# The inverse column transform of a spectral mix: half as many matmul columns, with two more levels of sums on VectorE and GpSimd

## The chip, the cores and the metric

The kernel runs on one core of one Trainium2 chip. A core has five engines that run side by side, each with its own instruction queue: TensorE (PE) for matmuls, VectorE (DVE), ScalarE (ACT) and GpSimd (POOL) for elementwise work, and SyncE (SP), which issues DMAs. They wait for each other through semaphores. The metric is the device time of one execution in microseconds; lower is better.

## The reference, cut to what matters

The input `x` is a float32 array of 16 batches, 16 channels and 256 x 256 points. Two layers follow each other, each behind a group normalisation and with a residual addition. The second is a stack of convolutions and a gate; the change doesn't touch it. The first is a layer in the frequency domain:

```python
alpha = jnp.fft.fft2(x, axes=(-2, -1))
...
S = jnp.einsum('ikpq,oikp,xikq->oxik', weights_residue, A, Bm)
output_residue1 = jnp.einsum('biox,oxik->bkox', alpha, S)
...
x1 = jnp.fft.ifft2(output_residue1, s=(Ny, Nx), axes=(-2, -1)).real
```

For every frequency (o, x) the 16 input channels are mixed into 16 output channels by a complex matrix `S`, which is made of poles and residues. The result goes back to space. The change lies in the part of the inverse transform that runs along x.

## The kernel before, in words

The program has four stages: `layer0_forward` (transform to frequencies), `layer0_mix` (the mix, and the way back along x), `layer0_back` (the way back along y, with the pole terms), and `layer1`. They pass arrays through DRAM: the mix reads the spectrum `al` and writes `hd`, which `layer0_back` reads.

All transforms are matmuls against tables of cosines and sines, made on the host as constants by `fourier_tables`. In `layer0_forward` the spectrum along x comes from the table `wxn`, in the mix the way back along x uses the table `ix`. Both belong together: they fix at which points in x the transform takes its origin.

`layer0_mix` works through 33 groups of four rows of frequencies (the last group has one row). Its order is written out by hand for PE, ACT, DVE and POOL; each of these engines carries out its instructions in the order of the program text. A group `g` goes like this:

- `poles` builds weights `lt` on DVE (L629) for the next group.
- `mix(s, y, between)`: for 256 frequencies in x, small matmuls (L665) of the matrices `s` with the spread spectrum `alb`, 8 blocks; ACT copies each block from PSUM to `y` (L672). At blocks 24 and 48 (`x0`) it carries on with the column transform of the row before, which was left over.
- Then for the rows f = 0 to 3 of the group: `turn` transposes `y` on PE (L681); half of the result is copied by DVE (L687), half by ACT (L685), to `yt`. `residues` makes the matrices `s` of the next group on PE (L643), copied by DVE (L651) and ACT (L653) in turn. `spread` multiplies the next spectrum into `alb`: the expansions, on DVE (L607: three for f = 0 to 2, one for f = 3) and ACT (L605: two for f = 0 to 2). Then `columns`, which the change rewrites. For f = 3 it is put off into the next mix loop.

The next mix can't begin before all of `s` and of `alb` are written. `alb` has one buffer, so its expansions begin after the mix that reads it.

`columns(g, f, yt)` takes the frequencies of one row and gives values at 256 points in x. The 16 batches are in two halves of lanes, q = 0 and 1, and the even and odd frequencies (e) are summed apart. For each e it has four products (real and imaginary input c; v) per half, accumulated in PSUM tile `ph[q]`: 16 matmuls with 256 columns each. In float32 each matmul is two instructions on PE in the profile, so 32 in a step. The first 128 points need even + odd, the other 128 even - odd: ACT copies the odd half out of PSUM (L709), DVE makes the sum (L712) and the difference (L713) into tile `h`, and POOL issues two DMAs that store `h` to `hd` (L720). The pool of `ph` has two buffers, that of `h` five.

Of the kernel before, what the change touches and what calls it, by code (L numbers as in the profile page):

```python
# [10 lines left out]
F32 = mybir.dt.float32  # L11
I32 = mybir.dt.int32
AF = mybir.ActivationFunctionType
ALU = mybir.AluOpType
# [5 lines left out]
N = 256  # L20
G = 8
P = 128
# [3 lines left out]
TWO_PI = 2.0 * np.pi  # L26
# [30 lines left out]
def load(nc, pool, src, shape, name):  # L57
    t = pool.tile(shape, F32, tag=name, name=name)
    nc.sync.dma_start(out=t, in_=src)
    return t  # L60
# [493 lines left out]
def layer0_mix(ctx, tc, d, al, hd, tabs):  # L554
# [3 lines left out]
    nc = tc.nc  # L558
    nb = d["x"].shape[0]
    cp = ctx.enter_context(tc.tile_pool(name="mc", bufs=1))  # L560
# [12 lines left out]
    for k in range(0, C, 4):  # L573
        nc.sync.dma_start(out=tt[:, :, k : k + 4], in_=tabs[0][:, :, k : k + 4])
    ident = load(nc, cp, d["ident"], [P, P], "ident")
    ix = load(nc, cp, d["ix"], [P, 8, N], "ix")

# [5 lines left out]
    hp = ctx.enter_context(tc.tile_pool(name="mh", bufs=3))  # L585
    psg = ctx.enter_context(tc.tile_pool(name="psg", bufs=4, space=PSUM))
    pst = ctx.enter_context(tc.tile_pool(name="pst", bufs=2, space=PSUM))
    psh = ctx.enter_context(tc.tile_pool(name="psh", bufs=2, space=PSUM))
# [85 lines left out]
    def turn(y, f):  # L674

        yt = hp.tile([P, 8, 8, C], F32, tag="yt", name="yt", bufs=2)
        for t0 in range(0, 8, 4):
            pt = pst.tile([P, 4, P], F32, tag="pt", name="pt")
            for t in range(4):
                j = 16 * f + 2 * (t0 + t)  # L680
                nc.tensor.transpose(pt[:, t], y[:, j : j + 2].rearrange("p q x -> p (q x)"), ident)  # L681
            dst = yt[:, :, t0 : t0 + 4].rearrange("p c t k -> p t c k")
            src = pt.rearrange("p t (c k) -> p t c k", k=C)
            if t0:
                nc.scalar.copy(dst, src)  # L685
            else:
                nc.vector.tensor_copy(dst, src)  # L687
        return yt

    def columns(g, f, yt):  # L690

        ph = [psh.tile([P, 2, N], F32, tag="ph", name="ph") for q in range(2)]
        for e in range(2):
            if e:
                yield
            for n, (c, v) in enumerate(((0, 0), (0, 1), (1, 0), (1, 1))):
                i = 2 * (2 * c + e) + v
                for q in range(2):
                    lanes = slice(64 * q, 64 * q + 64)
                    nc.tensor.matmul(  # L700
                        ph[q][:, e],
                        lhsT=yt[lanes, i].rearrange("p t k -> p (t k)"),
                        rhs=ix[lanes, i],
                        start=n == 0,
                        stop=n == 3,
                    )
        for q in range(2):
            odd = hp.tile([P, 2, P], F32, tag="odd", name="odd", bufs=2)
            nc.scalar.copy(odd, ph[q][:, 1].rearrange("p (v x) -> p v x", v=2))  # L709
            o = hp.tile([P, 2, 2, P], F32, tag="h", name="h", bufs=5)  # L710
            even = ph[q][:, 0].rearrange("p (v x) -> p v x", v=2)
            nc.vector.tensor_tensor(o[:, :, 0], even, odd, ALU.add)  # L712
            nc.vector.tensor_tensor(o[:, :, 1], even, odd, ALU.subtract)  # L713
            o = o.rearrange("p v h x -> p v (h x)")
            fy = 4 * g + f
            for v in range(2):

                if fy % P or v == 0:
                    part = fy // P if fy % P == 0 else v
                    nc.gpsimd.dma_start(  # L720
                        out=hd[fy % 2, part, fy % P // 2, q:nb:2].rearrange("b k x -> b (k x)"),
                        in_=o[:, v],
                    )

    E = mybir.EngineType
    with tc.manual_schedule(engines={E.PE, E.Activation, E.DVE, E.Pool}):
# [3 lines left out]
        s = gp.tile([P, N, 2, C], F32, tag="s", name="s")  # L730
# [7 lines left out]
        for g in range(NF):  # L738
            more = g + 1 < NF
            y = gp.tile([P, 64, 64], F32, tag="y", name="y")  # L740
            if more:
                lt = poles(av)
            mix(s, y, between)
            if more:
                s = gp.tile([P, N, 2, C], F32, tag="s", name="s")
                residues(lt, s, 0)
            for f in range(4 if more else 1):
                if more and f == 3:
                    spread(spectrum, f)
                    for k0 in (12, 14):  # L750
                        residues(lt, s, k0)
                yt = turn(y, f)
                if more:
                    for k0 in range(2 if f == 0 else 4 * f, 4 * f + 4, 2) if f < 3 else ():
                        residues(lt, s, k0)
                    if f < 3:
                        spread(spectrum, f)
                    if g + 2 < NF:
                        if f == 0:
                            av = load_poles(g + 2)  # L760
                        spectrum[f] = load_spectrum(g + 2, f)
                between = columns(g, f, yt)
                if f < 3:
                    for _ in between:
                        pass
# [642 lines left out]
def fourier_tables():  # L1408

    k = np.arange(N)  # L1410
    turns = np.outer(k, k) % N * (TWO_PI / N)
    cos, sin = np.cos(turns), np.sin(turns)

    def parities(a):
        return a.reshape(P, 2, *a.shape[1:])


    fy = np.stack([np.stack([cos[:P, e::2][:, :64], -sin[:P, e::2][:, :64]], 1) for e in (0, 1)], 1)
    fy[:, 0, 1, 0] = cos[:P, P]
    wx = np.stack([cos, -sin, sin], axis=1)  # L1420

    wxn = np.stack(
        [
            np.stack([np.concatenate([cos[:P, e::2], -sin[:P, e::2]], 1),
                      np.concatenate([sin[:P, e::2], cos[:P, e::2]], 1)], axis=1)
            for e in (0, 1)
        ],
        axis=1,
    )

    ix = np.stack([np.concatenate(a, 1) for a in ((cos[:, :P], sin[:, :P]), (-sin[:, :P], cos[:, :P]))], 1)
    ix = np.tile(ix.reshape(64, 8, N), (2, 1, 1))

    iy = np.stack([cos[:P], -sin[:P]], axis=1) / (N * N)
    iy[0, 0] *= 0.5
    iy[0, 1] = 0.5 * cos[P] / (N * N)
    number = (k + P) % N - P
    mirrored = -number[-k % N]
    ii, tt = np.arange(C), np.arange(2)

    mt = np.zeros((2, C, M, 2, 2, 8))
    for t in tt:
        for i in ii:
            mt[t, i, :, i // 8, t, i % 8] = 1
    out = {
        "fy": fy.reshape(P, 2, P),
        "wx": parities(wx),
        "wxa": parities(wx[..., :P]),
        "wxn": wxn,
        "ix": ix,  # L1450

        "iy": iy[..., :P].reshape(64, 2, 2, P).transpose(2, 0, 1, 3).reshape(P, 2, P),
        "ones": np.full((P, P), 1.0 / P),
        "pair": np.stack([np.tile(np.eye(64), (2, 1)), -np.tile(np.eye(64), (2, 1))], axis=1),
        "gc": np.tile(np.repeat(np.eye(G), 2, axis=0), (8, 1)),
        "ident": np.eye(P),
        "kcol": parities(number),
        "krow_t": np.repeat(np.stack([number, mirrored]), 64, axis=0),
        "krow_m": np.tile(np.repeat(np.stack([number, mirrored]), 32, axis=0), (2, 1)),
        "sign_t": np.repeat([-1.0, 1.0], 64)[:, None],  # L1460
        "sign_m": np.tile(np.repeat([-1.0, 1.0], 32), 2)[:, None],
        "mk": np.tile(np.repeat(np.eye(C), M, axis=0), (2, 1)),
        "m4": np.tile(np.repeat(np.eye(4), 8, axis=0), (4, 1)),
        "m8": np.tile(np.repeat(np.eye(8), M, axis=0), (4, 1)),
        "mt": mt.reshape(P, 2, 16),
        "phase": np.repeat([0.25, 0.0], 64)[:, None],
        "last": np.repeat([0.5, -0.5], 64)[:, None] / (N * N),
    }
    return {name: a.astype(np.float32) for name, a in out.items()}
# [70 lines left out]
```

## Time and profile before

| what | value |
|---|---|
| median of 3 runs | 7066.57 us (7063.95 to 7071.69) |
| profiled execution, its span | 7064.8 us |
| busy, share of the span | PE 93%, DVE 79%, ACT 54%, POOL 50% |
| mean granted PE clock | 0.976 |
| mix, first to last group of four rows | 1413 to 2880 us |
| L700, matmuls of `columns` | 4128 instructions, 509.6 us busy, 393 ns mean |
| L712 and L713, sum and difference | 258 each, medians 425 and 415 ns |
| L709, copy on ACT | 258, median 378 ns |
| L607, expansions on DVE | 330, median 1392 ns |
| L720, store issues on POOL | 512, median 596 ns |

The span is the time from the first to the last instruction of the one execution that the profiler recorded; 1.8 us lie between it and the median. [...] "Idle before, releaser" tells what an engine waited for; "issue" stands for a wait in which the profile sees no releaser. Lines such as L700 are lines of the program.

### The profile page before, as it was taken

The numbers are of one execution on the slowest core, as the hardware profiler recorded it, in microseconds if no ns is written. First come the engines' busy times: TensorE is split into PE (matmuls) and PEld (weight loads), VectorE is DVE, ScalarE is ACT, GpSimd is POOL, SyncE is SP. The second block draws the span as 40 slices with busy tenths as digits, with TensorE's granted clock in tenths as the row PEclk, the third lists the DMA queues.
The fourth block names the chain that finished last, engine by engine and source line by source line (L and its number), as shares of the span: only waits on it lengthen the run. The fifth ranks groups of instructions, "written<-read, shape, count | busy, mean of one in ns | idle before, by whom it ended". The sixth has DMA issues, their size and how long they took to land. (4 is left out here: it accounts for less than half of the span.)

```text
span 7064.8 us, 144662 instructions
## 1 busy us (share of the span) xinstructions
PE 6544.4 (93%) x55592; PEld 3663.8 (52%) x55592; DVE 5610.5 (79%) x10346; ACT 3836.7 (54%) x5996; POOL 3516.5 (50%) x4614
## 2 busy tenths in 40 slices
PE   7889999899999999899979999999999999999996
PEld 5777778677677677677723333333333333333331
DVE  8999985466666666688878888888888888888885
ACT  1223333366666666322266666676666666666671
POOL 2334445412222222466655666667666667665663
PEclk9899999999999999999989999999999999999998
DMA  3334444433333333699968888899888889888886
GB/s 97 112 114 124 121 126 124 131 96 97 96 102 99 100 95 100 211 326 327 326 188 251 261 257 267 277 277 286 272 258 265 275 276 285 270 260 264 279 271 212
DMA packets 716083, 1443.41 MB, mean 204 GB/s; under 512 B 98954, under 2 KB 525254, under 8 KB 673638
## 3 DMA queue, kind: packets, MB, share of 16 engines
q1 hardware_dynamic: 567206, 959.76, 44.3%
q0 software_dynamic: 148192, 474.40, 21.4%
q8 instruction: 444, 7.27, 0.4%
q14 instruction: 241, 1.97, 0.1%
HBM read 877.12 MB, written 556.47 MB: 203 GB/s over the span
## 5 line engine op out<-in xcount | busy, mean ns | idle before, releaser
L1087 ACT ACTIVATE wide<-c,b 32x512 f32<-32x512 f32 x2176 | 1477.5, 679 | 312.8 <-PE c L1039 264.1
L1118 DVE TENSOR_TENSOR top<-pd,t 32x512 f32<-32x512 f32 x2176 | 1504.3, 691 | 52.5
L1039 PE MATMUL c<-z,w 102*128 102x512 f32 x2048 | 999.5, 620 | 110.5 <-ACT wide L1087 89.0
L1115 DVE TENSOR_TENSOR t<-pd,r 64x512 f32<-64x512 f32 x1088 | 744.4, 684 | 349.6 <-PE pd L1107 311.9
L1099 POOL COPY wide<-wide 32x1031 f32<-32x1031 f32 (+1 forms) x576 | 577.9, 1003 | 886.8 <-ACT wide L1087 859.7
L1107 PE MATMUL pd<-wide,dw 128*128 128x512 f32 x2048 | 990.9, 605 | 12.0 <-DVE top L1118 11.0
L720 POOL DMA_DIRECT2D hd<-h x512 | 323.3, 638 | 1192.5 <-DVE h L713 1169.0
L1039 PEld LDWEIGHTS c<-z,w 102*128 102x128 f32 x2048 | 371.7, 192 | 697.5 <-issue 460.1
L1187 PE MATMUL c2ps<-rows,c 128*32 128x512 f32 x6144 | 721.8, 602 | 5.6 <-DVE odd L1214 5.6
L1107 PEld LDWEIGHTS pd<-wide,dw 128*128 128x128 f32 x2048 | 381.8, 192 | 572.5 <-issue 420.2
L1058 ACT ACTIVATE bot<-c,b 128x512 f32<-128x512 f32 x544 | 344.0, 683 | 464.5 <-issue 382.7
L1100 POOL COPY wide<-wide 32x1031 f32<-32x1031 f32 (+1 forms) x576 | 576.9, 1002 | 33.5
L700 PE MATMUL ph<-ix,yt 64*128 64x256 f32 x4128 | 509.6, 393 | 10.7 <-issue 9.9
L643 PE MATMUL ps<-tt,lt 128*64 128x256 f32 x4224 | 493.2, 384 | 10.4 <-DMA tt<-td 9.2
L313 PE MATMUL px<-wxn,u 128*64 128x256 f32 x4224 | 481.6, 379 | 8.0 <-ACT o L320 8.0
L207 PE MATMUL pu<-fy,eo 128*128 128x128 f32 x2048 | 428.6, 293 | 25.4 <-DVE u L224 21.3
L700 PEld LDWEIGHTS ph<-ix,yt 64*128 64x128 f32 x4128 | 397.0, 191 | 99.3 <-issue 51.3
L1187 PEld LDWEIGHTS c2ps<-rows,c 128*32 128x32 f32 x6144 | 175.9, 108 | 513.5 <-issue 402.3
L875 POOL TENSOR_TENSOR x<-x,o 128x512 f32<-128x512 f32 x256 | 324.0, 1266 | 217.8 <-DVE o L874 199.8
L607 DVE TENSOR_SCALAR alb<-alc,m 128x1024 f32<-128x1024 f32 x330 | 419.6, 1395 | 0.0
L214 PE MATMUL pv<-at,eo 128*128 128x128 f32 x2048 | 415.5, 286 | 0.0
L651 DVE COPY s<-ps 128x512 f32<-128x512 f32 x264 | 266.3, 1027 | 183.3 <-PE ps L643 166.3
(220 smaller groups left out, 11728.0 us busy)
## 6 DMA issues: line engine op xcount, KB each, us to landing
rows<-cf SPq DMA_DIRECT2D x128, 2176.0 KB
z<-zn SPq DMA_DIRECT2D x768, 257.8 KB
cf<-top POOLq DMA_DIRECT2D x512, 240.0 KB, 6.8
cf<-bot POOLq DMA_DIRECT2D x96, 840.0 KB, 11.0
alc<-al SPq DMA_DIRECT2D x264, 256.0 KB
zn<-zb SPq DMA_DIRECT2D x128, 516.0 KB
o<-zn SPq DMA_DIRECT2D x128, 516.0 KB
z<-in_x SPq DMA_DIRECT2D x64, 1024.0 KB
```

The costliest lines, as they stand in the source:

```text
L207: nc.tensor.matmul(pu[:, xh, e].rearrange("p v m -> p (v m)"), lhsT=lhs, rhs=fy[:, e], start=True, stop=True,)
L313: nc.tensor.matmul(ps[64 * k : 64 * k + 64, :, h], lhsT=u[:, h, part, g0 + j + k].rearrange("p f c -> p (f c)"), rhs=wxn[:, h, part], star ...
L643: nc.tensor.matmul(ps[64 * h : 64 * h + 64, v], lhsT=lt[:, h, k, 1 - v : 3 - v].rearrange("p l f c -> p (l f c)"), rhs=tt[:, h, k], start= ...
L700: nc.tensor.matmul(ph[q][:, e], lhsT=yt[lanes, i].rearrange("p t k -> p (t k)"), rhs=ix[lanes, i], start=n == 0, stop=n == 3,)
L1039: nc.tensor.matmul(ps[:, a], lhsT=w, rhs=z[:k, c : c + 2, 0:N], start=True, stop=True)
L1087: nc.scalar.activation(self.feat[64 - 32 * q : 96 - 32 * q, f, self.groups[g], :H], ps[q][32 * f : 32 * f + 32], AF.Mish, bias=b1[0][32 * ...
L1099: nc.gpsimd.tensor_copy(flat[0:32, f, 1:m], flat[64:96, f, 0 : m - 1])
L1100: nc.gpsimd.tensor_copy(flat[96:128, f, 0 : m - 1], flat[32:64, f, 1:m])
L1107: nc.tensor.matmul(ps, lhsT=dwt if self.tail else dw, rhs=self.feat[:, f, cs, :H], start=True, stop=True,)
L1115: nc.vector.tensor_tensor(t[64:128], ps[:64], self.r[:, cs], ALU.mult)
L1118: nc.vector.tensor_tensor(self.top[32 * f : 32 * f + 32, cs, q], ps[lanes], t[lanes], ALU.add)
L1187: nc.tensor.matmul(ps[32 * j : 32 * j + 32], lhsT=w[:, blk], rhs=src[:, 4 * j + blk : 4 * j + blk + 4, x : x + H], start=(i, blk) == (0, 0 ...
```

## The change

The way back along x is now taken on a grid moved by half a sample. The forward table `wxn` uses the angles of (2k + 1) instead of 2k, and `ix` likewise. On such a grid, the points x and 255 - x are mirror images: the cosine part has the same value at both, and the sine part the opposite one. The points x and x + 128 still differ only in the sign of the odd frequencies. So `ix` needs 64 points instead of 128, with a block of cosines and one of sines.

The matmuls of `columns` have 128 columns instead of 256. They are as many as before, each output now takes two products instead of four, and the output goes into two of four blocks of 64 in `ph` for each e: blocks 0 and 3 for v = 0, blocks 1 and 2 for v = 1. ACT copies the antisymmetric blocks (`anti`). DVE makes `w`: symmetric + antisymmetric, and symmetric - antisymmetric, the latter written backwards in x. POOL, which did nothing but issue the stores here, then makes the sum and the difference over e into `h`: two instructions for each half. The stores stay. The tile `w` is new (three buffers of 2 KB a partition), and `ix` has half its size.

```diff
-    ix = load(nc, cp, d["ix"], [P, 8, N], "ix")
+    ix = load(nc, cp, d["ix"], [P, 8, P], "ix")
...
-        ph = [psh.tile([P, 2, N], F32, tag="ph", name="ph") for q in range(2)]
+        ph = [psh.tile([P, 2, 4, 64], F32, tag="ph", name="ph") for q in range(2)]
         for e in range(2):
             if e:
                 yield
-            for n, (c, v) in enumerate(((0, 0), (0, 1), (1, 0), (1, 1))):
-                i = 2 * (2 * c + e) + v
-                for q in range(2):
-                    lanes = slice(64 * q, 64 * q + 64)
-                    nc.tensor.matmul(
-                        ph[q][:, e],
-                        lhsT=yt[lanes, i].rearrange("p t k -> p (t k)"),
-                        rhs=ix[lanes, i],
-                        start=n == 0,
-                        stop=n == 3,
-                    )
+            for v in range(2):
+                blocks = slice(0, 4, 3) if v == 0 else slice(1, 3)
+                for c in range(2):
+                    i = 2 * (2 * c + e) + v
+                    for q in range(2):
+                        lanes = slice(64 * q, 64 * q + 64)
+                        nc.tensor.matmul(
+                            ph[q][:, e, blocks],
+                            lhsT=yt[lanes, i].rearrange("p t k -> p (t k)"),
+                            rhs=ix[lanes, i].rearrange("p (b x) -> p b x", b=2),
+                            start=c == 0,
+                            stop=c == 1,
+                        )
         for q in range(2):
-            odd = hp.tile([P, 2, P], F32, tag="odd", name="odd", bufs=2)
-            nc.scalar.copy(odd, ph[q][:, 1].rearrange("p (v x) -> p v x", v=2))
-            o = hp.tile([P, 2, 2, P], F32, tag="h", name="h", bufs=5)
-            even = ph[q][:, 0].rearrange("p (v x) -> p v x", v=2)
-            nc.vector.tensor_tensor(o[:, :, 0], even, odd, ALU.add)
-            nc.vector.tensor_tensor(o[:, :, 1], even, odd, ALU.subtract)
-            o = o.rearrange("p v h x -> p v (h x)")
+            anti = hp.tile([P, 2, 2, 64], F32, tag="anti", name="anti", bufs=2)
+            nc.scalar.copy(anti, ph[q][:, :, 2:])
+            w = hp.tile([P, 2, 2, 2, 64], F32, tag="w", name="w")
+            sym = ph[q][:, :, :2]
+            nc.vector.tensor_tensor(w[:, 0], sym, anti, ALU.add)
+            nc.vector.tensor_tensor(w[:, 1, :, :, ::-1], sym, anti, ALU.subtract)
+            o = hp.tile([P, 2, 4, 64], F32, tag="h", name="h", bufs=5)
+            parts = o.rearrange("p v s x -> p s v x")
+            nc.gpsimd.tensor_tensor(parts[:, 0::3], w[:, :, 0], w[:, :, 1], ALU.add)
+            nc.gpsimd.tensor_tensor(parts[:, 2:0:-1], w[:, :, 0], w[:, :, 1], ALU.subtract)
+            o = o.rearrange("p v s x -> p v (s x)")
...
+    half = np.outer(2 * k + 1, k) % (2 * N) * (TWO_PI / (2 * N))
+    cosh, sinh = np.cos(half), np.sin(half)
     wxn = np.stack(
...
-            np.stack([np.concatenate([cos[:P, e::2], -sin[:P, e::2]], 1),
-                      np.concatenate([sin[:P, e::2], cos[:P, e::2]], 1)], axis=1)
+            np.stack([np.concatenate([cosh[:P, e::2], -sinh[:P, e::2]], 1),
+                      np.concatenate([sinh[:P, e::2], cosh[:P, e::2]], 1)], axis=1)
...
-    ix = np.stack([np.concatenate(a, 1) for a in ((cos[:, :P], sin[:, :P]), (-sin[:, :P], cos[:, :P]))], 1)
-    ix = np.tile(ix.reshape(64, 8, N), (2, 1, 1))
+    ch, sh = cosh.T[:, :64], sinh.T[:, :64]
+    ix = np.stack([np.concatenate([ch, sh], 1), np.concatenate([ch, -sh], 1)], 1)
+    ix = np.tile(ix.reshape(64, 8, P), (2, 1, 1))
```

## The prediction

> **What bounds the kernel now.** First the windows view, to find the stage. The changed function runs in the mix, 1413 to 2907 us: 33 groups, of which 32 whole ones take 1466.6 us, 45.8 us each. The second line is what follows a group's mix loop: four rows of residues, turns and columns, 30.6 us.
>
> ```profile
> core 0: us, PE busy (x) PEld busy (x) DVE busy (x) ACT busy (x) POOL busy (x), PEclk, DMA share, GB/s
> 1413.40:2880.00 1466.60, 1353.22 (x25568) 1027.04 (x25569) 991.70 (x1404) 912.35 (x1086) 319.78 (x506) 0.98 0.33 97
> 2023.73:2054.30 30.57, 29.72 (x266) 21.25 (x261) 25.70 (x35) 23.77 (x25) 9.79 (x16) 1.00 0.40 110
> ```
>
> PE is busy for 97% of those 30.6 us, but DVE for 84% and ACT for 78%. So the second question is how far behind PE the others are. The timeline of one step (row f=1; start, length, engine, line) answers it.
>
> ```profile
> 2036.79 3.73 PE L700 MATMUL ph<-ix,yt 64*128 64x256 f32 x32
> 2040.44 1.09 PE L681 MATMUL pt<-ident,y 128*128 128x128 f32 x8
> 2041.47 3.67 PE L643 MATMUL ps<-tt,lt 128*64 128x256 f32 x32
> ...
> 2037.79 3.77 DVE L607 TENSOR_SCALAR alb<-alc,m 128x1024 f32<-128x1024 f32 x3
> 2041.36 0.42 DVE L712 TENSOR_TENSOR h<-ph,odd 128x256 f32<-128x256 f32 x1
> 2041.72 0.39 DVE L713 TENSOR_TENSOR h<-ph,odd 128x256 f32<-128x256 f32 x1
> ...
> 2042.38 0.40 DVE L713 TENSOR_TENSOR h<-ph,odd 128x256 f32<-128x256 f32 x1
> 2042.71 0.66 DVE L687 COPY yt<-pt 128x512 f32<-128x512 f32 x1
> 2043.46 1.03 DVE L651 COPY s<-ps 128x512 f32<-128x512 f32 x1
> 2045.19 1.03 DVE L651 COPY s<-ps 128x512 f32<-128x512 f32 x1 [0.69 <-PE ps L643]
> ```
>
> A step lasts 8.28 us (2036.79 to 2045.07) and PE has no gap in it. DVE by start-to-start distances: expansions 3.57, sums and differences 1.35, turn copy 0.75, two residue copies 0.88 each: 7.43 us. Its only idle time is the 0.69. ACT by the same count (two expansions 3.85, the rest 3.2): about 7.1. PE is the bound, DVE stands 0.85 us behind it.
>
> **What the change saves on PE.** The 32 column instructions run as 16 pairs, one on each half of the rows; a pair starts every 216 ns for 256 columns (3.45 us of the 3.73). Is the weight load the limit for 128 columns? Two views: four loads of 187 ns within 0.30 us, so the two halves load together; and L207/L214 with 128 columns and 128x128 weights, two instructions every 0.22 us, 112 ns each.
>
> ```profile
> 2001.41 0.30 PEld L700 LDWEIGHTS ph<-ix,yt 64*128 64x128 f32 x4 [0.39 <-issue]
> ...
> 1022.98 0.39 PE L207 MATMUL pu<-fy,eo 128*128 128x128 f32 x2
> 1023.20 0.39 PE L214 MATMUL pv<-at,eo 128*128 128x128 f32 x2
> ```
>
> [...] A pair then takes 112 ns: 16 x 104 = 1.66 us less a step, 6.65 a group, 215 us over 129 steps. Were the loads serial, it would be about 0; the four in 0.30 us speak against that.
>
> **What of it passes DVE.** DVE's counts and sizes stay: four operations of 256 elements a step, one of them written backwards. I take it at the present 0.33 to 0.36 us; the trace has no reversed write: 0 to +0.3 us each, so 0 to +1.8 a group on DVE. ACT's copy keeps its size (0.35 to 0.39 us). I walked one group (mix start 2010.60 is 0; the next now starts at 43.67). The two halves of the deferred column step lie inside the mix loop, so residues start 1.66 earlier, at 11.46; the first DVE expansions at 17.24 instead of 18.91. From there DVE never waits again: 3.56 + 1.35 + 0.75 + 0.88 + 0.88 twice, then 3.56 + 1.35 + 1.24 (the lone expansion of row 3) + 1.76 puts the last residue copy at 40.2, and the next mix, which needs all of s, at 40.3. So of PE's 6.65 us only 3.4 can arrive: 1.66 in the mix loop, 1.7 after it. PE waits for DVE in the rest. The DMAs of spectra follow the expansions and move with them; ix is half as large, loaded once, about nothing.
>
> **What it adds on GpSimd.** Two TENSOR_TENSORs of 128x256 per half, four a step, 516 in all. L265 is that shape:
>
> ```profile
> 118.76 0.72 POOL L265 TENSOR_TENSOR acc<-acc,t 128x256 f32<-128x256 f32 x1 [3.43 <-DVE t L252]
> ```
>
> 2.9 us a step beside four store issues of 0.60: with the waits between, 5.9 of some 8 us. As busy time it is no bound. But it shares something with DVE. [...] The trace agrees in three places: the table's L517, normally 0.49 us, took 1.56 behind a GpSimd TENSOR_TENSOR; the second of three store issues, beside an expansion L607, took 1.27 instead of 0.60; and L1177, normally 1.37, stayed out until three of four GpSimd instructions in a row were through.
>
> ```profile
> 550.73 2.37 POOL L194 TENSOR_TENSOR eo<-z 128x1024 f32<-128x1024 f32 x1 [3.95 <-PE pv L214]
> 551.82 1.56 DVE L517 TENSOR_SCALAR n<-arg,phase 128x512 f32<-128x512 f32 x1
> ...
> 1454.23 2.45 POOL L720 DMA_DIRECT2D hd<-h  x3 [5.92 <-DVE h L713]
> 1454.52 1.43 DVE L607 TENSOR_SCALAR alb<-alc,m 128x1024 f32<-128x1024 f32 x1
> ...
> 4000.03 3.29 POOL L1255 TENSOR_SCALAR o<-o,scale,mean 128x258 f32<-128x258 f32 x4
> 4000.25 2.63 DVE L1177 TENSOR_TENSOR pair<-rows 128x1161 f32<-128x1161 f32 x1
> ```
>
> So the DVE expansions meet the new GpSimd work. Let T be the end of the first half's w. GpSimd: sums T+0.1 to 1.5, its two stores, which wait for them, to 3.2, the second half's sums 3.2 to 4.7, stores to 6. DVE: w of the second half to T+0.65, copies [...] to 3.1, then three expansions in a row to 6.7. The second half's two sums fall into the expansions: they cost DVE up to 2 x 0.72 = 1.4 us, at least 1.0 if the first is under way. That happens before rows 1 and 2. In row 3 the lone expansion comes at T+0.65, between the first half's sums: 0.85. Row 0 is spared: the mix loop lies between. Sum 2.9 to 3.7 a group if the lock acts as above, 0 if it does not; I take 3.05. Behind a blocked expansion queue the next w, the turn copy and the residue copies; for the turn copy PE's columns wait, for the residue copies the next mix.
>
> Hidden parts: the anti copy on ACT is ahead of DVE. A w buffer is used again three halves later, about 12 us, after its sums. The store's later start (1.5 to 3 us) matters only at the stage's end, where the next stage reads hd: +3 us, once.
>
> **Two effects in the mix loop.** PE would now stand idle about 5 us ahead of each mix. After such a gap the present trace shows half a clock:
>
> ```profile
> 2378.79 0.86 PE L665 MATMUL pg<-alb,s 128*32 128x64 f32 x22 [4.63 <-issue]
> ...
> 2378.80:2383.30 4.50, 4.50 (x39) 3.14 (x38) 0.00 (x0) 0.58 (x1) 0.00 (x0) 0.50 0.01 4
> ```
>
> [...] Price 0 to 2.3 us a group. Against it: every mix loop already has gaps of 1 to 4.8 us that nothing on the page releases ("issue"), the loop's mean is 15.3 us and its shortest 12.9. If PE lacks instructions there, a slower clock costs less, but a shorter column step also gains less. I let 1.66 gained end as 0.3 (between +1.66 and -0.7).
>
> **Sum.** Per group -1.7 (after the loop) -0.3 (loop) +3.05 (lock) = +1.05; 32 groups +34, end of the stage +3: the profiled execution's 7064.8 becomes 7102. The median of the runs shown is 1.8 above that span: 7103.
>
> **Rivals.** (a) The lock does not bite: GpSimd's sums slip between the expansions[...]. For it: L607 has no long instance so far (1.35 to 1.49), though only store issues met it. Against: the 1.27 us issue. Then -2.5 to -3.4 a group, 6958 to 6990. It decides when the lock costs under 1.6 us a group. (b) Lock and gain cancel: lock 2 to 2.5, 7052 to 7081. (c) The backward write is slow and the clock halves fully: another +1.5 to +3 a group, 7150 to 7200. (d) PE's whole gain arrives, -6.65 a group: 6855; DVE's 7.43 of 8.28 us speaks against it.
>
> **Chances.** Forecast 0.55 (7081 to 7150), (a) 0.20, (b) 0.15, (c) 0.07, (d) 0.03. A measurement of this kernel tells 0.2%, 14 us, from no change: faster 0.23, same 0.15, slower 0.62. The range 6972 to 7155 leaves out (d), the best of (a), most of (c). The forecast's own is 7081 to 7150.
>
> **What would show it.** Column pairs every 112 ns, L700 near 2 us a step; if not, the PE step is wrong. L607 means well above 1.39 us, with GpSimd sums beside them; if they stay, rival (a). PE waiting for the turn copy and, for several us, ahead of each mix; PEclk under 0.95 there. The reversed w no slower than the plain one. Wrong would be: an order of grants that always lets DVE first, or a mix loop that gains its full 1.66.

## The result and the profile after

The changed kernel takes 7085.1 us (median of 14 runs, 7072.79 to 7093.16) beside 7066.21 us for the kernel before on the same chip (14 runs, 7059.87 to 7071.69). The ratio is 1.0026 with a 95% interval of 1.0019 to 1.0033: slower by 0.26%. The forecast was slower by 0.52%, 7103 us. The direction was right and the range held; the forecast size was nearly twice the measured one (36.4 beside 18.9 us).

The profiled execution took 7093.16 us, the longest of the 14. Its span is 7091.4 us, 26.6 more than before, while the medians differ by 18.9. So sums made from the two profiles come to 26.6, and some 8 us of that belong to this one execution.

First the windows view of the changed kernel's mix, 32 whole groups; the columns are window, length, then busy time and instructions of PE, weight load, DVE, ACT and GpSimd, then PE's clock, DMA share and GB/s.

```profile
core 0: us, PE busy (x) PEld busy (x) DVE busy (x) ACT busy (x) POOL busy (x), PEclk, DMA share, GB/s
1418.00:2911.10 1493.10, 1200.71 (x25568) 945.01 (x25569) 1069.01 (x1404) 900.25 (x1086) 837.70 (x1012) 0.93 0.33 95
```

PE lost 152 us of busy time (1353.22 before), and the stage became 26.5 us longer: 46.66 us a group instead of 45.83. DVE has the same 1404 instructions, but 77 us more busy time. GpSimd went from 320 to 838 us.

Where DVE's time went shows in the timeline of one step (row f=1, then the lone expansion of row 3): start, length, engine, line, and in brackets the idle time before.

```profile
1721.48 2.06 PE L702 MATMUL ph<-ix,yt 64*128 64x128 f32 x32
1741.21 5.00 PE L665 MATMUL pg<-alb,s 128*32 128x64 f32 x182 [4.81 <-DVE s L651]
...
1715.71 3.80 DVE L607 TENSOR_SCALAR alb<-alc,m 128x1024 f32<-128x1024 f32 x3
1723.02 4.72 DVE L607 TENSOR_SCALAR alb<-alc,m 128x1024 f32<-128x1024 f32 x3
1727.54 0.44 DVE L714 TENSOR_TENSOR w<-ph,anti 128x256 f32<-128x256 f32 x1
1727.91 0.40 DVE L715 TENSOR_TENSOR w<-ph,anti 128x256 f32<-128x256 f32 x1
1737.17 2.20 DVE L607 TENSOR_SCALAR alb<-alc,m 128x1024 f32<-128x1024 f32 x1
...
1721.88 1.20 POOL L726 DMA_DIRECT2D hd<-h  x2 [0.30 <-POOL h L719]
1723.09 1.75 POOL L718 TENSOR_TENSOR h<-w 128x256 f32<-128x256 f32 x1
1724.82 1.69 POOL L719 TENSOR_TENSOR h<-w 128x256 f32<-128x256 f32 x1
1726.81 1.67 POOL L726 DMA_DIRECT2D hd<-h  x2 [0.30 <-POOL h L719]
```

The column step is 2.06 us instead of 3.73. The chain of three expansions at 1715.71 (row 0, spared) takes 3.80 us; the one at 1723.02 (row 1) takes 4.72. The two sums of the second half are issued at its start and last 1.75 and 1.69 us instead of 0.73: each waits for an expansion to end, gets in, and the next expansion waits for it. The second and third expansion of that chain by themselves:

```profile
1724.21 1.86 DVE L607 TENSOR_SCALAR alb<-alc,m 128x1024 f32<-128x1024 f32 x1
1725.88 1.86 DVE L607 TENSOR_SCALAR alb<-alc,m 128x1024 f32<-128x1024 f32 x1
```

Alone an expansion takes 1.39 us. So sums and expansions alternate. The subtraction that is written backwards (L715) takes 0.40 us, the plain sum before it (L714) 0.44.

PE's waits in the mix stage (us in total, times, longest), first in the kernel before, then in the changed one:

```profile
PE pg L665 <- issue: 71.1, 38, 4.8
PE pg L665 <- DVE s L651: 26.4, 31, 0.9
```

```profile
PE pg L665 <- DVE s L651: 149.0, 31, 5.4
PE pg L665 <- issue: 67.0, 69, 3.1
PE ph L702 <- DVE yt L687: 48.4, 32, 2.0
```

Ahead of each mix PE now waits 4.8 us for the last residue copy; before, it was 26.4 us in total. The 71.1 us of waits without a releaser that the kernel before had inside its mix loops are nearly all still there.

Four quantities are compared below, as means over the 32 groups: a group's period, its mix loop (first to last L665), the rest, and the chains of expansions in rows 1 and 2 and the lone one in row 3.

| us | group | loop | rest | row 1 | row 2 | lone |
|---|---|---|---|---|---|---|
| before | 45.83 | 15.30 | 30.53 | 3.77 | 3.76 | 1.45 |
| after | 46.66 | 15.31 | 31.35 | 4.75 | 4.84 | 2.13 |
| sums left out | 43.28 | 14.73 | 28.55 | 3.80 | 3.79 | 1.38 |
| sums of both halves first | 44.35 | 14.90 | 29.45 | 3.81 | 4.63 | 1.40 |
| before + sums | 45.90 | 14.96 | 30.93 | 3.87 | 3.98 | 1.56 |
| PE kept busy | 46.10 | 14.62 | 31.48 | 4.75 | 4.83 | 2.18 |
| no spectrum loads | 45.51 | 14.17 | 31.33 | 4.75 | 4.84 | 2.13 |
| stores on SP | 43.41 | 14.68 | 28.72 | 3.84 | 3.79 | 1.48 |
| stores on SP, again | 43.49 | 14.77 | 28.72 | 3.84 | 3.79 | 1.48 |
| the same, 7 matmuls in the gap | 43.82 | 15.01 | 28.81 | 3.84 | 3.80 | 1.52 |
| before, stores on SP | 45.92 | 15.34 | 30.58 | 3.77 | 3.77 | 1.40 |

Each row is one execution. The first two come from one chip, the others from chips on which the kernel before took 7054 to 7057 us instead of 7066; no profile of it from there is kept. The rest and the chains repeat well: 30.53 and 30.58, 31.35 and 31.33, 28.72 twice, in rows that should agree there. The loop does not: 9 to 12 us between chips would be up to 0.4 us a group if they lay in it. So a difference of the loop between chips is read with a margin of 0.4 us. The ratios below are free of this: each is to the kernel before, run again on the same chip.

### The profile page after: what moved, and what is told of

It is laid out like the page before. It is cut to its first block, busy times and chain, and to the rows that moved or that the text cites. A ratio compares the mean times of both kernels' runs of the same rounds, so it can differ in the third digit from the quotient of the medians.

```text
span 7091.4 us, 145084 instructions
## 1 busy us (share of the span) xinstructions
PE 6396.4 (90%) x55592; PEld 3587.7 (51%) x55592; DVE 5687.6 (80%) x10346; ACT 3824.5 (54%) x5996; POOL 4047.2 (57%) x5130
## 4 chain that ended last, share of the span: by engine, by line
PE 69%; DVE 20%; issue 4%; ACT 4%; DMA 2%; SPq 0%; POOL 0%; ACTq 0%; DVEq 0%; POOLq 0%
PE c2ps L1193 16%; PE c L1045 13%; PE pd L1113 13%; PE pg L665 5%; PE ps L643 3%; PE px L313 3%; DVE alb L607 3%; PE ph L702 3%; ACT wide L1093 3%; PE pu L207 2%; PE pv L214 2%; PE py L868 2%; PE pr L1072 2%; PE py L869 2%; DVE s L651 2%
## 5 line engine op out<-in xcount | busy, mean ns | idle before, releaser
L718 POOL TENSOR_TENSOR h<-w 128x256 f32<-128x256 f32 x258 | 252.1, 977 | 613.5 <-DVE w L715 610.5
L665 PE MATMUL pg<-alb,s 128*32 128x64 f32 x16896 | 347.4, 251 | 242.0 <-DVE s L651 153.9
L607 DVE TENSOR_SCALAR alb<-alc,m 128x1024 f32<-128x1024 f32 x330 | 508.6, 1667 | 0.0
L665 PEld LDWEIGHTS pg<-alb,s 128*32 128x32 f32 x16896 | 319.0, 132 | 270.4 <-issue 262.0
L726 POOL DMA_DIRECT2D hd<-h x512 | 358.4, 704 | 87.1 <-POOL h L719 74.5
```

The lines of the kernel that those rows point to most:

```text
L607: eng.tensor_scalar(dst, t, m4[:, j : j + 1], None, ALU.mult)
L665: nc.tensor.matmul(ps[32 * q : 32 * q + 32, x], lhsT=s[:, i].rearrange("p v k -> p (v k)"), rhs=alb[:, i].rearrange("p j b -> p (j b)"), s ...
```

## The experiments

The theory is the prediction's: the shorter columns would pay, but the sums on GpSimd hold up the expansions (the lock). The rivals: DVE's new form costs it, PE's clock costs it, or something other than the sums does.

### The sums left out

```diff
...
-            nc.gpsimd.tensor_tensor(parts[:, 0::3], w[:, :, 0], w[:, :, 1], ALU.add)
-            nc.gpsimd.tensor_tensor(parts[:, 2:0:-1], w[:, :, 0], w[:, :, 1], ALU.subtract)
-            o = o.rearrange("p v s x -> p v (s x)")
+            o = w.rearrange("p i e v x -> p i (e v x)")
```

> The changed kernel without the two GpSimd sums: the stores take w as it is, so the last sums and differences over the frequency parity are left out. Matmuls, ACT copy, DVE operations and the four stores of a step stay. Theory [...]: the chains of three expansions in rows 1 and 2 fall from 4.74 and 4.80 us back to 3.8, the lone one of row 3 from 2.2 to 1.45, a group from 46.7 to 43.9 us or less; 32 groups: about 88 us under the changed kernel, 6997 us. Rival (slow clock and gaps in the mix loop eat the gain, the lock is without effect on the end): the chains get shorter, but a group stays at 46 us or more, 7065 to 7085 us.

6978.8 us, ratio 0.9895 (0.9880 to 0.9910). The chains are back at 3.8 us and the group is 3.38 us shorter than with the sums, 2.80 of that outside the loop. Row 1's chain in this kernel:

```profile
1483.63 3.79 DVE L607 TENSOR_SCALAR alb<-alc,m 128x1024 f32<-128x1024 f32 x3
```

From ratio to ratio the sums cost 1.3%, 93 us or 2.9 a group, so nearly all of it lies outside the loop. Column matmuls, the reversed write and PE's gap ahead of each mix (3.0 us here) are still in, so none of them alone makes the change slow: the sums do, and without them the change would gain 1.05%.

### The sums of both halves ahead of all four stores

```diff
+        made = []
         for q in range(2):
...
-            o = o.rearrange("p v s x -> p v (s x)")
-            fy = 4 * g + f
+            made.append(o.rearrange("p v s x -> p v (s x)"))
+        fy = 4 * g + f
+        for q, o in enumerate(made):
             for v in range(2):
```

> The changed kernel with one change of order on GpSimd: the four sums of a step first, then its four stores. Theory [...]: the sums now lie from 0.1 to 2.9 us after the first w, the expansions of rows 1 and 2 begin at 3.1, so their chains fall to 3.8; the lone expansion of row 3 stays at about 2.2. That is 2.0 us a group, 65 us: 7020 us, faster than the kernel before. Rival (it is GpSimd's amount of work, not its place): 7085 us, no change.

7014.28 us, ratio 0.9944 (0.9930 to 0.9959). Row 1 is free, as expected, but row 2 is not (4.63 us) and the lone expansion is (1.40): both were expected the other way round. The timeline of this kernel, GpSimd and then DVE, shows why:

```profile
1479.50 5.80 POOL L728 DMA_DIRECT2D hd<-h  x4
1485.32 0.74 POOL L719 TENSOR_TENSOR h<-w 128x256 f32<-128x256 f32 x1
...
1487.40 1.70 POOL L720 TENSOR_TENSOR h<-w 128x256 f32<-128x256 f32 x1
...
1479.59 3.79 DVE L607 TENSOR_SCALAR alb<-alc,m 128x1024 f32<-128x1024 f32 x3
1486.88 4.64 DVE L607 TENSOR_SCALAR alb<-alc,m 128x1024 f32<-128x1024 f32 x3
```

Four store issues meet row 1's chain and take 5.80 us; elsewhere in the same trace four take 2.39. The chain itself is not delayed (3.79 us). Here a store issue waited for the whole chain, where a sum in the changed kernel got in after one expansion (1.75 us, 0.73 of it its own). But row 2's sums, whose first input is ready at 1484.0, begin behind the stores at 1485.32, and the last two of the four meet the next chain: the third sum delays its first expansion (1.78 us instead of 1.39), the fourth its second (1.85). That chain costs 0.85 us more. So GpSimd's stores cost DVE nothing and still bring the next sums to the wrong place.

### The kernel before with two sums a half added

```diff
+            w = hp.tile([P, 2, 2, P], F32, tag="w", name="w", bufs=1)
+            nc.gpsimd.tensor_tensor(w[:, 0], o[:, :, 0], o[:, :, 1], ALU.add)
+            nc.gpsimd.tensor_tensor(w[:, 1], o[:, :, 0], o[:, :, 1], ALU.subtract)
```

The sums are extra work whose result nobody reads.

> The kernel before, with two GpSimd sums of the same size for each half added after its sum and difference; their results go to a tile that nobody reads. Matmuls stay at 256 columns. Theory [...]: expansions get longer as in the changed kernel, by 0.8 to 1 us in rows 1 and 2 and 0.7 in row 3; DVE has 0.85 us of slack in a step, so about 0.1 us shows in rows 1 and 2, and 0.7 in row 3, ahead of the mix: 0.8 to 1.2 us a group, 7092 to 7105 us. Rival (sums are harmless): 7066 us, and L607 at 1.40 us.

7066.11 us, ratio 1.0019 (1.0012 to 1.0025), and the chains only 0.1 to 0.2 us longer: the expected lock did not appear. The time after the loop is 0.40 us a group longer, as much as the three chains together (0.43); times 32 that is the 13 us of the ratio. (The loop of this row, 0.34 us shorter, is from another chip than the kernel before.) Its timeline:

```profile
1483.62 0.74 POOL L716 TENSOR_TENSOR w<-h 128x256 f32<-128x256 f32 x1
1484.30 4.40 POOL L723 DMA_DIRECT2D hd<-h  x2
...
1484.12 3.85 DVE L607 TENSOR_SCALAR alb<-alc,m 128x1024 f32<-128x1024 f32 x3
```

In the kernel before PE is the bound, so DVE waits 0.68 us for the residues before its last copy and the expansions begin later; and here the stores do not wait for the sums. The last sum ends 0.2 us into the chain; then two store issues stand through it (4.40 us instead of 1.20). In the changed kernel DVE no longer waits at that place, and the first half's stores wait 0.30 us for their sums: together 1.0 us, and both sums of the second half fall into the chain. This explanation is read from two timelines, not tested on this kernel. That timing decides in the changed kernel, and not the sums as such, is what the stores on SP test below.

### PE kept busy ahead of each mix

After the last row's `turn`, 15 matmuls whose result nobody reads fill PE's gap:

```diff
+                if more and f == 3:
+                    spare = [psh.tile([P, 2, 4, 64], F32, tag="ph", name="ph") for q in range(2)]
+                    for i in range(15):
+                        nc.tensor.matmul(
+                            spare[i % 2][:, 0].rearrange("p s x -> p (s x)")[:, :P],
+                            lhsT=ident, rhs=ix[:, i % 8], start=True, stop=True)
```

> The changed kernel with 15 matmuls of 128 columns on PE, whose results nobody reads, after the last turn of each group, where PE now idles 4.8 us. Rival theory (slow clock): after the gap PE runs at half clock for about 4.3 us, worth up to 2 us a group; with the gap filled the mix loop falls from 15.3 to about 13.3 us, 60 us in all: 7025 us. Theory ([...]the loop is also held by gaps without a releaser): 0 to 1 us a group, 7055 to 7085 us.

7068.81 us, ratio 1.0021 (1.0012 to 1.0031): not to be told from the changed kernel's 1.0026. In the changed kernel the clock read 0.50 for 4.5 us on average (2.5 to 11.7) after 31 gaps of 4.4 to 4.9 us ahead of a mix; with the gap filled PE's mean clock rises from 0.964 to 0.977, and the wait for DVE ahead of the mix is all but gone:

```profile
PE pg L665 <- issue: 101.8, 82, 4.5
PE pg L665 <- DVE s L651: 15.5, 29, 0.6
```

But the waits without a releaser rise from 67.0 to 101.8 us, 1.1 us a group. The loop is 0.69 us shorter than the changed kernel's, on another chip; the two ratios leave room for about 0.2 us of that (0.1 a group in all, with 0.13 lost after the loop).

### No loads of spectra in the mix

```diff
-                        spectrum[f] = load_spectrum(g + 2, f)
+                        pass
```

From the third group on the mix takes old spectra; the loads are what is left out. Do they lengthen the loop's gaps?

> The changed kernel without the spectrum loads of groups 2 to 32: the expansions read the spectrum of group 1 again and again, so 124 loads of 0.5 MB are left out. Theory [...]: the loops of over 17 us vanish, the mean falls from 15.3 to 14 to 14.5 us, but gaps of about 1 us stay. Rival (the gaps come from PE alone): the loop stays at 15.3 us.

One execution: 7051.34 us (before on that chip 7057.1). The loop is 1.14 us shorter (by the times, about 0.75), the rest unchanged (31.33), and the waits without a releaser fall from 67.0 to 45.5 us over the same groups, the longest from 3.1 to 1.8. So the loads lengthen those gaps, as far as one execution tells. What the gaps are is told less surely. In the trace of before, each of the 44 PE gaps over 0.9 us in the mix stage ends 1.1 to 1.7 us after a 16 KB transfer on the queue that the profile calls instruction (q8) has landed. A group has about six such transfers. In the trace of the changed kernel the same holds for all 36 gaps over 0.9 us without a releaser, and for none of the 64 that end with a copy of DVE. Whether PE stands without instructions there was not shown: no run took these transfers away.

### The stores on SP

```diff
-                    nc.gpsimd.dma_start(
+                    nc.sync.dma_start(
                         out=hd[fy % 2, part, fy % P // 2, q:nb:2].rearrange("b k x -> b (k x)"),
```

> The changed kernel with the stores of the mix issued by SP instead of GpSimd; GpSimd has only the sums left. Theory (a store issue that meets a chain of expansions is held until its end, and the sums queue behind it): all four sums of a step are now over before the next chain begins, so the chains of rows 1 and 2 are 3.8 us, the lone expansion of row 3 stays at 2.1 to 2.2; a group about 44.2 us, ratio to the kernel before 0.991 to 0.993. Rival (SP holds the stores back behind its loads, h buffers run out, GpSimd waits): a group at 46 us or more, ratio 1.00 or above.

6985.84 us, ratio 0.9896 (0.9881 to 0.9911), and on another occasion:

> The changed kernel with its stores on SP once more, on the chip of this comparison: ratio to before 0.988 to 0.991 as found, a group 43.4 us, 28.7 us of it after the loop.

6986.08 us, ratio 0.9900 (0.9885 to 0.9915). The group is that of the kernel without sums (43.41 beside 43.28 us). The timeline, GpSimd and then DVE:

```profile
1520.77 0.73 POOL L718 TENSOR_TENSOR h<-w 128x256 f32<-128x256 f32 x1 [8.60 <-issue]
...
1522.84 0.74 POOL L719 TENSOR_TENSOR h<-w 128x256 f32<-128x256 f32 x1
...
1523.59 3.78 DVE L607 TENSOR_SCALAR alb<-alc,m 128x1024 f32<-128x1024 f32 x3
```

Four sums run back to back and are through when the chain begins. The lone expansion was expected at 2.1 to 2.2 us and took 1.48: here it gets in between two sums and the second sum waits. In the changed kernel both sums go first at nearly the same distance (expansion issued 0.40 us after the first sum there, 0.45 us here). Why the order differs stays open; with it the run came out better than the 0.991 to 0.993 that were expected.

Two more kernels belong to this. Does the move of the stores pay by itself? The same edit on the kernel before:

> The kernel before, with only the stores of hd moved from POOL's queue to SP's. Theory (the move pays because it frees GpSimd's sums from the expansions, and the kernel before has no sums): time within 0.2% of before, chains of three expansions 3.75 to 3.8 us and a group 45.6 to 46.0 us as before. Rival (issuing the stores on POOL costs time in itself, so part of the 1.04% is not the change's): ratio under 0.997, a group under 45.5 us.

7065.58 us, ratio 1.0012 (1.0004 to 1.0021); chains and group as before. The move gains nothing without the change; if anything it loses 0.1%. And with the lone expansion moved in front of row 3, into row 2's chain:

```diff
-        (((3, 0), (3, 1)), ((2, 2), (2, 3), (3, 2))),
-        ((), ((3, 3),)),
+        (((3, 0), (3, 1)), ((2, 2), (2, 3), (3, 2), (3, 3))),
+        ((), ()),
```

> As the run with stores on SP, and the lone expansion of row 3 moved to the end of the chain of row 2, where no sum is under way. Theory [...]: chain of row 2 at 5.0 us with four expansions, no expansion over 1.5 us, a group 43.3 us as without the sums, ratio 0.989 to 0.990: the GpSimd sums cost nothing any more. Rival (another cost of the sums than the lock, such as the later store): 44 us or more, ratio 0.993 or above.

6994.91 us, ratio 0.9908 (0.9894 to 0.9923): nothing gained, since the lone expansion was nearly free already (1.48 us).

### The gap filled again, with the lock gone

> As the run before it, with the 15 unread matmuls of 128 columns ahead of each mix. Theory ([...]a faster clock is eaten by longer gaps): a group within 0.5 us of the run without them, ratio 0.988 to 0.991, and the gaps without a releaser grow by some 30 us. Rival (slow clock): loop 1.5 us shorter, ratio 0.983 or below.

The last kernel plus the 15 matmuls: 7022.08 us, ratio 0.9944 (0.9927 to 0.9961). The loop is 0.57 us shorter than in that kernel (14.51 beside 15.08), but the rest 1.57 us longer (30.17 beside 28.60), where at most 0.5 for the whole group was expected. The waits without a releaser, expected to grow by 30 us, grew only from 91.8 to 97.3. A likely cause: with the lock gone the gap is only 3 us, and the matmuls run past it. To separate that, the kernel with stores on SP got 7 matmuls instead of 15:

> The changed kernel with stores on SP, and 7 instead of 15 unread matmuls in PE's gap ahead of each mix, so that they end about 0.9 us before s is ready. Theory (the 15 lost time because they ran past the gap): the time after the loop falls back to 28.5 to 29.0 us a group, the loop is 14.2 to 14.6 us as with 15, because its gaps without a releaser grow to 85 to 105 us; ratio to the version without them 0.998 to 1.000. Rival 1 (unread matmuls cost in another way): over 29.4 us after the loop. Rival 2 (the clock's gain arrives once nothing overshoots): loop under 13.6 us, ratio 0.994 or less to the version without them.

7002.31 us, ratio 0.9920 (0.9905 to 0.9935); 16 us over the version without them on the same chip, where no more than equal was expected. The rest falls back to 28.81 us, as the theory had it. But the loop does not get shorter: 15.01 us beside 14.77, where 14.2 to 14.6 was expected. PE's waits without these matmuls, then with them:

```profile
PE pg L665 <- DVE s L651: 98.7, 32, 3.1
PE pg L665 <- issue: 78.4, 72, 3.6
```

```profile
PE pg L665 <- issue: 112.8, 86, 3.7
PE pg L665 <- DVE s L651: 49.8, 32, 1.6
```

PE's clock rises from 0.971 to 0.976, and the gaps inside the loop grow by 34 us, 1.1 a group, so the loop gains nothing from it. Such gaps differ between runs without the matmuls too (73.7, 78.4 and 91.8 us in three), so the cause of the 34 us isn't shown. What is shown is the time: in none of three kernels did filling PE's gap pay clear of the noise.

## Why the prediction had the direction right and the size wrong

**PE's column step** was forecast at -1.66 us and is -1.67 (3.73 to 2.06), with a pair of matmuls every 112 ns as forecast. The two halves load their weights together here too: two loads of 188 ns (median) within 0.22 us at 1721.45.

**DVE as the next bound** was right in kind. PE waits 1.55 us for the turn copy (in the step shown, and 48.4 us altogether) and 4.8 us ahead of each mix; about 5 was forecast. Without the sums the time after the loop is 1.98 us shorter, where 1.7 was taken. Rival (d), the whole PE gain, is out.

**The reversed write** costs nothing: a mean of 413 ns beside 417 for the plain difference before. Rival (c) falls with it.

**The lock** was right as to cause and place: rows 1 and 2 and the lone expansion, row 0 spared. Sized at 1.1 + 1.1 + 0.85 = 3.05 us, it measured 0.98 + 1.08 + 0.68 = 2.74. A sum adds about 0.5 us to a chain rather than its 0.72. In the chain at 1723.02 the first sum got in after one expansion (1.75 us with its wait), and the next expansion took 1.86 us instead of 1.39. A store issue got in only after the last: two took 4.40 us beside a chain in the kernel before with sums. The lone expansion went the other way: begun at 1737.17, 0.29 us before the second sum, it took 2.20 us, and that sum its usual 0.73. The copies out of PSUM were not held up: the turn copy at 1720.65 took 0.69 us beside two sums of 0.72 and 0.73, and in the mix stage the means are 672 ns for L687 (675 before) and 1033 for L651 (1027). The traces show these delays; what GpSimd and VectorE share was not shown. Rival (a) needs the lock under 1.6 us and falls, for the order of this kernel; with the stores on SP it is what happens.

**The mix loop** was taken at -0.3 and measured 0.0 (15.31 beside 15.30), inside its bounds. Its argument, that gaps of its own swallow both most of the 1.66 us and most of what the slow clock costs, is not contradicted, but its parts were not measured one by one. In the kernel before, the clock read 0.50 for 5.6 to 5.9 us after three of the four longest waits inside the loops (3.40, 4.61 and 4.63 us), and for 3.4 us after the one that ends at 1735.8 (4.82). It also did so for 3.4 us within 1.4 us of the end of seven shorter waits (1.76 to 2.45 us), but stayed at 1.00 after three of 2.57 to 2.88.

**The end of the stage** was taken at +3 us once. The record can't tell this. From the last group's start to the end of the kernel the profile after has 4.5 us less than before, and up to the first mix 4.6 more; but single executions differ by as much: the other nine runs with the changed tables reach the first mix at 1410.6 to 1415.4 us and the two others without them at 1411.2 and 1415.6, and from the last group to the end all of them take 4179 to 4191.

**What failed is one term of the sum, the time after the loop: the lock's +3.05 less the gain of 1.7.** It was put at +1.35 us a group and measured +0.82 (30.53 to 31.35). Both parts were off, in the same direction: the sums cost 2.80 us after the loop (31.35 less the 28.55 without them; 2.74 by the chains), and the gain was 1.98. Of the lock, the waits in the chains and most of all the lone expansion's were priced too high; why the gain was larger stays open. Over 32 groups that is 43 us forecast and 26 measured, and these 17 us are what the forecast lies too high on the medians (36.4 beside 18.9). All other terms together were put at -0.3 x 32 + 3 = -7 us, and 18.9 - 26 leaves -7. That this agrees so well is in part luck: in the two profiled executions, whose spans differ by 26.6, those terms add up to nothing. Since gain and lock nearly cancel, an error of a tenth in either moves the answer by a third.

Rival (b) deserves a second reading. By the prediction's own sum a lock of 2 to 2.5 us gives 7070 to 7086, not the 7052 to 7081 written there; the measured 7085 lies between forecast and rival, not clearly with the one.

## What to carry to other kernels

When an operation moves to GpSimd, look not at how full GpSimd is but at what runs on VectorE at the moment it is issued: here about 1 us of timing went with the difference between a sum that was nearly free and one that cost half a microsecond. Where GpSimd computes beside such chains, try its store issues on another queue: here they were held through a whole chain of expansions (four in 5.80 us instead of 2.39), and the next sums came late into the next chain; on SP the same stores made a loss of 0.26% into a gain of 1.0%, the best version of this study. And before paying for a faster clock or fewer columns inside a loop, read how much of the loop is gaps that nothing releases.

## What was not expected of the hardware

- In a chain of three expansions a GpSimd sum waited for one of them (1.75 us, of it 0.73 its own), but GpSimd's store issues waited for all three: two took 4.40 us instead of 1.20, four 5.80 instead of 2.39.
- In the mix stage of the kernel before, PE's gaps over 0.9 us end 1.1 to 1.7 us after a 16 KB transfer on the instruction queue, q8 (44 of 44). With matmuls filling the gap ahead of the loop the waits without a releaser were larger in two of three kernels (67.0 to 101.8 us, 78.4 to 112.8; but 91.8 to 97.3), and smaller with data loads left out (67.0 to 45.5, one execution).
